# Linear attention stack: a block's projections issued beside another block's attention

## The chip, the cores and the metric

One NeuronCore of a Trainium2 chip runs the whole kernel. The metric is the device time of one execution in microseconds (us), as the median of several runs; the profile comes from one further execution. TensorE is PE in the profile (PEld is its weight load), VectorE is DVE, ScalarE is ACT, GpSimd is POOL, and SyncE (SP) issues most transfers.

## The reference, cut to what matters

A batch of 2 sequences of 2048 positions with 256 features goes through a stack of three layers with causal linear attention (16 heads of 16), and then through two layers with windowed softmax attention. All is float32. The change touches the first stack alone:

```python
for l in range(L):                       # L = 3
    q = (out @ Wq[l] + bq[l]).reshape(B, S, N_HEAD, dh)
    k = (out @ Wk[l] + bk[l]).reshape(B, S, N_HEAD, dh)
    v = (out @ Wv[l] + bv[l]).reshape(B, S, N_HEAD, dh)
    Qf = favor(q, omega[l])              # exp(+-u - |x|^2/2), u = x @ omega
    Kf = favor(k, omega[l])
    a = causal_linear_attention(Qf, Kf, v).reshape(B, S, D)
    a = a @ Wo[l] + bo[l]
    h = layer_norm(out + a, ln1_g[l], ln1_b[l])
    y = jax.nn.relu(h @ W1[l] + bf1[l]) @ W2[l] + bf2[l]
    out = layer_norm(h + y, ln2_g[l], ln2_b[l])
...
# causal_linear_attention, per head and position:
#   S += k v^T ; z += k ; out = (q S) / (q z + eps)
```

## The kernel before, in words

The stack cuts each sequence into 8 blocks of 256 positions: 16 blocks, each with 3 layers, so 48 layer steps. `favor_block` (L732) is one block's whole way and `favor_layer` (L462) one layer of it. Both are Python generators: the code up to the next `yield` issues a piece of work, and the `yield` says how much TensorE time the piece is counted for, how long the block has then to wait for other engines, which key it needs for its next piece, and which other layer step must be done before. `planned` (L91) holds four blocks at a time (`at_once`) and lets the one go on that is due first and whose key is free. A key is held by one block at a time. The order that comes out is the order of TensorE's instructions; those of the other engines are put in order by the framework, from the same program. Every engine then works through its own list.

The pieces of a layer, with the names of their tiles, as the profile shows them:

- projections: `pq` (L475) for q and k, `pv` (L491) for v, then `xs` on DVE (L486) with its squares on ACT (L487), and `vp` on DVE (L502)
- features: `pu` (L516), a product that uses the array in two column halves (128*64 in the profile), `ft` = exp on ACT (L526), `qe` on DVE (L532)
- scores: the running sum `z` (DVE L538, POOL L548), the transposes `tk` (L552) and their copy `ktm` (ACT L554), the first half of the scores `sc` (L563, rows in quarters, 32*128), masked to `att` by DVE (L569), the state update `su` (L583), masked to `sum` (DVE L591)
- second half of the scores, `den` (L611) and its reciprocal `rb` on ACT (L613, L614)
- values: `nd` from the states (L622) and from the weighted values (L635, the array in four column strips, 128*32), then `aT` on DVE (L658)
- output product `po` (L665), then the sum `s` (DVE L673) and a norm: statistics (L414, L415) on DVE, `rs` on ACT (L417, L418), `dn` on DVE (L421)
- `ntp` (L431) turns `dn`, ACT scales it (L435), POOL makes the residual `res` (L444, L445)
- the MLP in 8 pieces under the key `mlp`: `pf` (L687), relu to `fr` on ACT (L695), `acc` (L698), and behind the last one `s` (DVE L710) with a norm and `ntp`

Before the change, a block took the key `attention` ahead of its projections and gave it up behind `nd`; the projections also waited for the same layer of the sequence's previous block, whose state they do not use but the scores and values do.

PSUM is given out by tags, in turn within a tag. `mm` has three banks for pq, pv, pu, tk, su, den, nd, po and ntp. `sc` has four: a half of the scores takes all four, one for each quarter i, and each `pf` takes the next one:

```python
scs = [psum.tile([P, KT, 2, P], F32, tag="sc", name="sc", bufs=4) for _ in range(4)]
...
pf = psum.tile([P, TA], F32, tag="sc", name="pf", bufs=4)
```

`acc` has one bank, `xs` two buffers (for q and for k), and `vp` is one of two tiles that layer steps use in turn.

Behind the stack follows the softmax part, whose order is written out in a table of times (`WHEN`); the change does not touch it. The tables for it are loaded and scaled (`next_weights`, L721, `scale_tables`, L170) while the last blocks of the stack run.

Of the kernel before, what the change touches and what calls it, by code (L numbers as in the profile page):

```python
# [39 lines left out]
def block_kernel(ctx: ExitStack, tc: tile.TileContext, t: dict, out: bass.AP):  # L40
# [47 lines left out]

    done = set()

    def planned(jobs, at_once):  # L91

        jobs, live, held, now, count = iter(jobs), [], {}, 0.0, 0
        while True:
            while len(live) < at_once:
                g = next(jobs, None)
                if g is None:  # L100
                    break
                live.append([now, count, g, None, None])
                count += 1
            if not live:
                return
            e = min(
                e[:2] + [e] for e in live
                if held.get(e[3], e) is e and (e[4] is None or e[4] in done)
            )[2]
            if e[3]:  # L110
                held[e[3]] = e
            step = next(e[2], None)
            keep = step[2] if step and len(step) > 2 else None
            for k in [k for k, o in held.items() if o is e and k != keep]:
                del held[k]
            if step is None:
                live.remove(e)
                continue
            now = max(now, e[0]) + step[0]
            e[0] = now + step[1]  # L120
            e[3:] = list(step[2:]) + [None] * (4 - len(step))


    WHEN = {
# [88 lines left out]
    with ExitStack() as c1:  # L213
# [9 lines left out]
        def load_x(b, n):  # L223
            xin = work.tile([P, NCA, D], F32, tag="xin", name="xin", bufs=3)
            nc.sync.dma_start(
                xin, x_in[b, n * TA : (n + 1) * TA, :].rearrange("(c p) d -> p c d", p=P)
            )
            return xin
# [180 lines left out]
        def normed(src):  # L409

            mv = sp.tile([P, NCA, 2], F32, tag="mv", name="mv")
            for c in range(NCA):
                bs = sp.tile([P, 6], F32, tag="bs", name="bs")
                nc.vector.bn_stats(bs, src[:, c, :])  # L414
                nc.vector.bn_aggr(mv[:, c, :], bs)  # L415
            rs = sp.tile([P, NCA], F32, tag="rs", name="rs")
            nc.scalar.activation(rs, mv[:, :, 1], AF.Ln, bias=eps_t)  # L417
            nc.scalar.activation(rs, rs, AF.Exp, scale=-0.5)  # L418
            dn = work.tile([P, NCA, D], F32, tag="dn", name="dn", bufs=3)
            for c in range(NCA):  # L420
                nc.vector.tensor_scalar(  # L421
                    dn[:, c, :], src[:, c, :], mv[:, c, 0:1], rs[:, c : c + 1], ALU.subtract, ALU.mult
                )
            return dn

        def turned(dn, dst, gain, bias):

            tp = mm_tile("ntp").rearrange("p (k c) -> p k c", k=KT)
            for kt in range(KT):
                for c in range(NCA):  # L430
                    nc.tensor.transpose(  # L431
                        tp[:, kt, c * P : (c + 1) * P], dn[:, c, kt * P : (kt + 1) * P], ident
                    )
            for kt in range(KT):
                nc.scalar.activation(dst[:, kt, :], tp[:, kt, :], AF.Identity, bias=bias(kt), scale=gain(kt))  # L435

        def scaled(dn, gi, bi, plus=None):

            r = work.tile([P, NCA, D], F32, tag="res", name="res", bufs=6)
            add = brow[:, bi, :].unsqueeze(1).to_broadcast([P, NCA, D])  # L440
            if plus is not None:
                nc.gpsimd.tensor_tensor(plus, plus, add, ALU.add)
                add = plus
            nc.gpsimd.tensor_tensor(r, dn, brow[:, gi, :].unsqueeze(1).to_broadcast([P, NCA, D]), ALU.mult)  # L444
            nc.gpsimd.tensor_tensor(r, r, add, ALU.add)  # L445
            return r
# [15 lines left out]
        def favor_layer(b, n, l, h, hres):  # L462
# [38 lines left out]
            for c in range(NCA):  # L501
# [3 lines left out]
                    bvb[:, l, :].rearrange("p (i q d) -> p i q d", q=2, d=16),  # L505
                    ALU.add,
                )
            yield 5.2, 0.6, "attention"
            if callable(hres):
                hres = hres()  # L510
            feat = []
# [203 lines left out]
            h2 = hp.tile([P, KT, TA], F32, tag="h", name="h2")  # L715
            turned(dn, h2, lambda k: v("g2", k), lambda k: v("b2", k))
            hres = scaled(dn, R_G2 + l, R_B2 + l)
            yield 0.5, 0.9, "attention", (b, n - 1, l + 1) if n else None
            return h2, hres

        def next_weights():  # L721

            late.append(0)
            if len(late) == B:
                attn_w[0] = load_attn(0)
                mlp_w[0] = load_mlp(0)
            elif len(late) == 2 * B:
                scale_tables(*attn_w[0][1:4])
# [3 lines left out]
        def favor_block(b, n):  # L732
            if (b, n) == (0, 0):
                dn, h = h_first
            else:
                dn = normed(early.pop((b, n)) if (b, n) in early else load_x(b, n))
                yield 0.0, 4.0
                h = hp.tile([P, KT, TA], F32, tag="h", name="h0")
                turned(dn, h, lambda k: mod[:, 1, k, b : b + 1], lambda k: mod[:, 0, k, b : b + 1])
            hres = partial(scaled, dn, R_G0 + b, R_B0 + b)  # L740
            if n > 0:
                hres = hres()
            yield 0.5, 0.9, "attention", (b, n - 1, 0) if n else None
            for l in range(LA):
                if l == 2 and n == S // TA - 1:
                    next_weights()
                h, hres = yield from favor_layer(b, n, l, h, hres)
            if n == S // TA - 1:
                next_weights()
            x1 = scaled(h, R_GE + b, R_BE + b, load_x(b, n))  # L750
            at = n * NCA % NCH
            blk = b, n * TA // TB
            nc.sync.dma_start(xmid[blk][:, at : at + NCA, :], x1)
            dn = normed(x1)
            yield 0.0, 7.0
            hm = hp.tile([P, KT, TA], F32, tag="hm", name="hm", bufs=1)
            turned(dn, hm, lambda k: mod[:, 4, k, b : b + 1], lambda k: mod[:, 3, k, b : b + 1])
            nc.sync.dma_start(hmid[blk][:, :, at * P : at * P + TA], hm)
            yield 0.5, 0.0

        with tc.manual_schedule(engines={mybir.EngineType.PE}):
            blocks = [favor_block(b, n) for n in range(S // TA) for b in range(B)]
            with tc.issue_after(last_first):
                planned(blocks[:1] + [rest_of_setup()] + blocks[1:], 4)
# [632 lines left out]
```

## Time and profile before

| | us |
|---|---|
| median of 3 runs | 2979.69 (2979.21 to 2981.54) |
| the profiled execution | 2982.33 |
| its span on the core | 2980.5 |
| start of the last `acc` of the linear stack | 1563.2 |
| one layer step of the steady run, po to po | 31.4 |
| matmul group of four, start to next start | 0.86 |

The profile gives busy time per engine, the instructions in order of time, and for each idle stretch of an engine what ended it. A line such as `pf L687 <- DVE att L569` says that the matmul of L687 could not start until DVE had finished its instruction of L569. Ends of matmuls are modelled, and matmuls overlap, so the pace is read from start to start.

### The profile page before, as it was taken

The page shows a single profiled execution, that of the slowest core. Times are in us where ns is not written, and L with a number is a line of the kernel's source. Part 1 is how long each engine was busy: PE and PEld are TensorE (multiplying, and loading weights), DVE is VectorE, ACT ScalarE, POOL GpSimd, SP SyncE. Part 2 cuts the span into 40 slices and gives each one's busy share as a digit, 9 for nine tenths or more (in the row PEclk, how much of TensorE's full clock was granted, in tenths as well). Part 3 has the DMA queues.
Part 4 walks back from the last instruction along what each step waited for, and adds up shares of the span by engine and source line. Part 5 has one row for each costly group of instructions (what it writes and reads, how often), then busy time and mean ns, then how long its engine had stood idle before and what let it go on. Part 6 is the DMA issues. An engine that isn't in the chain of part 4 may idle for free.

```text
span 2980.5 us, 49140 instructions
## 1 busy us (share of the span) xinstructions
PE 2909.9 (98%) x19323; PEld 2128.4 (71%) x19323; DVE 1681.2 (56%) x4186; ACT 1339.6 (45%) x3263; POOL 1067.1 (36%) x942
## 2 busy tenths in 40 slices
PE   8999999999999999999996999999999999999999
PEld 6888887888888888888784777775444777776444
DVE  5555556555665556655534777774224777775222
ACT  3343344343443334343334667665114666766211
POOL 4222233222422223322324666663002666663000
PEclk9999999999999999999998999999999999999999
DMA  6000010000100001001012000001000000000011
GB/s 217 1 1 1 8 36 15 1 1 1 43 16 1 1 1 36 22 1 43 23 34 77 1 1 1 1 1 58 0 0 10 20 1 1 2 1 8 28 43 36
DMA packets 38327, 59.48 MB, mean 20 GB/s; under 512 B 3854, under 2 KB 29008, under 8 KB 37456
## 3 DMA queue, kind: packets, MB, share of 16 engines
q1 hardware_dynamic: 36288, 52.37, 5.3%
q8 instruction: 153, 2.51, 0.3%
q0 software_dynamic: 992, 2.92, 0.3%
q10 hardware_dynamic: 816, 1.05, 0.1%
q14 instruction: 78, 0.64, 0.1%
HBM read 43.72 MB, written 12.60 MB: 19 GB/s over the span
## 4 chain that ended last, share of the span: by engine, by line
PE 89%; DVE 4%; ACT 3%; POOL 2%; issue 1%; DMA 1%; ACTq 0%; POOLq 0%; DVEq 0%; SPq 0%
PE acc L698 11%; PE pf L687 10%; PE pqkv L860 10%; PE pg L1205 5%; PE pq L475 5%; PE acc L1243 5%; PE pa L1205 4%; PE av L1049 4%; PE sim L956 3%; PE ptp L1023 3%; PE po L1068 3%; PE nd L635 3%; PE sc L563 3%; PE pu L516 3%; PE po L665 3%; PE pv L491 3%
## 5 line engine op out<-in xcount | busy, mean ns | idle before, releaser
L698 PE MATMUL acc<-wb,fr 128*128 128x256 f32 x1536 | 398.5, 382 | 7.0 <-ACT fr L695 5.1
L687 PE MATMUL pf<-h,wa 128*128 128x256 f32 x1536 | 402.4, 385 | 0.6 <-DVE att L569 0.3
L695 ACT ACTIVATE fr<-pf,vec 128x256 f32<-128x256 f32 x384 | 180.6, 471 | 427.1 <-PE pf L687 426.3
L860 PE MATMUL pqkv<-wqkv,s 128*128 128x512 f32 x768 | 357.3, 601 | 6.5 <-DMA s<-h 6.5
L569 DVE TENSOR_TENSOR att<-sc,cst 128x512 f32<-128x512 f32 x384 | 238.3, 683 | 158.0 <-PE sc L563 158.0
L698 PEld LDWEIGHTS acc<-wb,fr 128*128 128x128 f32 x1536 | 288.8, 190 | 54.0 <-ACT fr L695 8.6
L444 POOL TENSOR_TENSOR res<-dn,brow 128x512 f32<-128x512 f32 x112 | 145.1, 1295 | 486.0 <-DVE dn L421 479.4
L687 PEld LDWEIGHTS pf<-h,wa 128*128 128x128 f32 x1536 | 277.3, 191 | 55.5 <-issue 19.8
L1011 POOL TENSOR_TENSOR pm<-pm,sum 128x1024 f32<-128x1024 f32 (+1 forms) x128 | 235.5, 1840 | 179.6 <-DVE sum L1006 179.6
L996 ACT ACTIVATE pm<-pm,mx 128x256 f32<-128x256 f32 (+1 forms) x512 | 249.4, 488 | 59.2 <-DVE mx L988 59.0
L860 PEld LDWEIGHTS pqkv<-wqkv,s 128*128 128x128 f32 x768 | 138.0, 193 | 133.9 <-issue 132.0
L902 POOL TENSOR_TENSOR rot<-raw,rsn_wo 128x512 f32<-128x512 f32 x128 | 160.3, 1273 | 180.8 <-ACT raw L883 180.5
L1214 DVE SCALAR_TENSOR_TENSOR ge<-pa,vec,ge 128x512 f32<-128x512 f32 x80 | 60.1, 751 | 282.9 <-PE pa L1205 231.6
L1213 ACT ACTIVATE ge<-pg,vec 128x512 f32<-128x512 f32 x96 | 65.8, 685 | 316.5 <-PE pg L1205 316.5
L487 ACT ACTIVATE xs<-xs 64x512 f32<-64x512 f32 x192 | 120.6, 628 | 152.3 <-DVE xs L486 143.0
L1205 PE MATMUL pg<-s,w 128*128 128x512 f32 (+1 forms) x384 | 182.2, 597 | 0.0
L475 PE MATMUL pq<-h,wa 128*128 128x256 f32 x768 | 176.2, 383 | 0.7 <-ACT h L435 0.7
L486 DVE TENSOR_TENSOR xs<-pq,vec 64x512 f32<-64x512 f32 x192 | 132.1, 688 | 75.3 <-PE pq L475 71.5
L1243 PE MATMUL acc<-ge,w 128*128 128x512 f32 (+1 forms) x384 | 168.8, 600 | 0.0
L475 PEld LDWEIGHTS pq<-h,wa 128*128 128x128 f32 x768 | 146.7, 192 | 22.6 <-issue 1.4
L924 POOL TENSOR_TENSOR qk<-qk,rot 128x1024 f32<-128x1024 f32 x64 | 151.3, 2363 | 0.5
L1205 PE MATMUL pa<-s,w 128*128 128x512 f32 x320 | 150.4, 592 | 0.0
(163 smaller groups left out, 5339.7 us busy)
## 6 DMA issues: line engine op xcount, KB each, us to landing
xin<-in_x_dram SPq DMA_DIRECT2D x32, 256.0 KB, 2.8
x<-res SPq DMA_DIRECT2D x16, 256.0 KB, 2.1
h<-hm SPq DMA_DIRECT2D x16, 256.0 KB, 2.4
s<-h SPq DMA_DIRECT2D x16, 256.0 KB, 4.8
xl<-x SPq DMA_DIRECT2D x8, 512.0 KB, 4.3
out_dram<-res SPq DMA_DIRECT2D x8, 512.0 KB, 3.2
w<-in_w_dram SPq DMA_DIRECT2D x6, 640.0 KB, 3.9
wa<-in_W_dram SPq DMA_DIRECT2D x3, 1024.0 KB, 8.3
```

The costliest lines, as they stand in the source:

```text
L475: nc.tensor.matmul(pq[:, g, :], W[wn, l][:, kt, g * P : (g + 1) * P], h[:, kt, :], start=(kt == 0), stop=(kt == KT - 1),)
L569: nc.vector.tensor_tensor(am, scs[i].rearrange("p g q c -> p (g q) c"), caus.unsqueeze(1).to_broadcast([P, 2 * KT, P]), ALU.mult,)
L687: nc.tensor.matmul(pf, W["W1", l][:, kt, f * P : (f + 1) * P], h1[:, kt, :], start=(kt == 0), stop=(kt == KT - 1),)
L695: nc.scalar.activation(fr[f], pf, AF.Relu, bias=v("bf1", f))
L698: nc.tensor.matmul(acc[:, c, :], fr[f - 1][:, c * P : (c + 1) * P], W["W2", l][:, f - 1, :], start=(f == 1 and c == 0), stop=(f == NF), sk ...
L860: nc.tensor.matmul(pq, s[:, kt * TB + c * P : kt * TB + (c + 1) * P], wqkv[:, kt, i * INNER : (i + 1) * INNER], start=(kt == 0), stop=(kt ...
L902: nc.gpsimd.tensor_tensor(rot[:, :, :, lo : lo + 32], got["raw"][:, :, :, hi : hi + 32], rsn[:, ti, :, lo : lo + 32].unsqueeze(2).to_broad ...
L924: nc.gpsimd.tensor_tensor(got["qk"], got["qk"], got["rot"], ALU.add)
L996: nc.scalar.activation(pm[:, hd, :], pm[:, hd, :], AF.Exp, bias=of("mx", hg)[:, hd : hd + 1], accum_out=of("sum", hg)[:, hd : hd + 1],)
L1011: nc.gpsimd.tensor_tensor(pm, pm, of("sum", hg).unsqueeze(2).to_broadcast([P, 4, kw]), ALU.mult)
L1205: nc.tensor.matmul(pt[:m, :], w1[:, kt, off : off + m], hb[:, kt * TB : (kt + 1) * TB], start=(kt == 0), stop=(kt == KT - 1),)
L1243: nc.tensor.matmul(acc[m], w2[rs_, f, m * P : (m + 1) * P], g[rs_, :], start=(f == 0), stop=(f == NFH - 1),)
```

## The change

Keys become sets. A block takes `projections` for its projections, and the wait for the previous block's layer step moves behind them: to the piece that makes the features, for which the block needs `projections` and `attention` together. After the features it gives `projections` up, so that another block may project while this one attends. A block that is due for `mlp` while another holds it brings the holder forward by `LEAD` (8 us of the planner's time). The last three places of the diff are, in order: behind the projections in `favor_layer`, at its end, and in `favor_block` ahead of the first layer.

```diff
+    LEAD = 8.0
+
     def planned(jobs, at_once):
...
-                live.append([now, count, g, None, None])
+                live.append([now, count, g, (), None])
                 count += 1
             if not live:
                 return
+
+            ahead = {
+                k for e in live for k in e[3]
+                if e[0] <= now and held.get(k, e) is not e and k == "mlp"
+            }
             e = min(
-                e[:2] + [e] for e in live
-                if held.get(e[3], e) is e and (e[4] is None or e[4] in done)
+                [e[0] - (LEAD if ahead & set(e[3]) else 0.0), e[1], e] for e in live
+                if all(held.get(k, e) is e for k in e[3]) and (e[4] is None or e[4] in done)
             )[2]
-            if e[3]:
-                held[e[3]] = e
+            held.update((k, e) for k in e[3])
             step = next(e[2], None)
-            keep = step[2] if step and len(step) > 2 else None
-            for k in [k for k, o in held.items() if o is e and k != keep]:
+            keep = step[2].split() if step and len(step) > 2 else ()
+            for k in [k for k, o in held.items() if o is e and k not in keep]:
                 del held[k]
...
-            e[3:] = list(step[2:]) + [None] * (4 - len(step))
+            e[3:] = keep, step[3] if len(step) > 3 else None
...
-            yield 5.2, 0.6, "attention"
+            yield 5.2, 0.6, "projections attention", (b, n - 1, l) if n else None
...
-            yield 0.5, 0.9, "attention", (b, n - 1, l + 1) if n else None
+            yield 0.5, 0.9, "projections"
...
-            yield 0.5, 0.9, "attention", (b, n - 1, 0) if n else None
+            yield 0.5, 0.9, "projections"
```

## The prediction

> **What bounds the kernel now.** I read the page first, then the busy time by stretches, then TensorE's waits, then the instructions of the linear stack in order of time.
>
> The page:
>
> ```profile
> span 2980.5 us, 49140 instructions
> PE   2909.9 (98%) x19323; PEld 2128.4 (71%) x19323; DVE 1681.2 (56%) x4186; ACT 1339.6 (45%) x3263; POOL 1067.1 (36%) x942
> ```
>
> TensorE is the bound. The change touches the linear stack alone, which ends at about 1565 us, and there TensorE is busy for 1537.5 of 1565 us; from 200 to 1400 us for 1192.5 of 1200, at a granted clock of 1.00. So this stage can gain only what TensorE loses between its matmuls, and it loses as soon as TensorE is made to wait. The view of its waits (columns: total us, times, longest) has little in that stack:
>
> ```profile
> PE ntp L431 <- DVE dn L421: 13.3, 4, 7.8
> PE acc L698 <- ACT fr L695: 5.1, 5, 1.2
> PE den L611 <- POOL z L548: 4.1, 1, 4.1
> PE tk L552 <- ACT ft L526: 3.1, 4, 0.9
> PE acc L698 <- DVE s L710: 1.8, 1, 1.8
> PE pf L687 <- DVE att L569: 0.3, 1, 0.3
> ```
>
> Now one layer step of the steady run, in order of time (start, us, engine, line). First TensorE, then VectorE (DVE):
>
> ```profile
> 599.90 1.03 PE L698 MATMUL acc<-wb,fr 128*128 128x256 f32 x4
> 600.86 1.95 PE L516 MATMUL pu<-xs,omt 128*64 128x256 f32 x16
> 602.73 1.13 PE L687 MATMUL pf<-h,wa 128*128 128x256 f32 x4
> 603.70 1.03 PE L698 MATMUL acc<-wb,fr 128*128 128x256 f32 x4
> 604.56 0.60 PE L552 MATMUL tk<-cst,ft 128*128 128x128 f32 x4
> 605.09 1.15 PE L563 MATMUL sc<-qe,ft 32*128 32x256 f32 x16
> 606.17 1.16 PE L583 MATMUL su<-vp,ktm 128*128 128x128 f32 x8
> 607.16 1.03 PE L687 MATMUL pf<-h,wa 128*128 128x256 f32 x4
> ```
>
> ```profile
> 606.26 2.48 DVE L569 TENSOR_TENSOR att<-sc,cst 128x512 f32<-128x512 f32 x4 [1.31 <-PE sc L563]
> 618.52 0.76 DVE L710 TENSOR_TENSOR s<-acc,res 128x256 f32<-128x256 f32 x2 [0.27 <-PE acc L698]
> 620.76 0.74 DVE L421 TENSOR_SCALAR dn<-s,mv,rs 128x256 f32<-128x256 f32 x2 [0.60 <-ACT rs L418]
> 621.41 0.75 DVE L673 TENSOR_TENSOR s<-po,res 128x256 f32<-128x256 f32 x2
> ```
>
> Start to start gives the pace: a group of four plain matmuls (acc at 603.70 to tk at 604.56) takes 0.86, but acc before pu takes 0.96, and pf after pu 0.97. Going into and out of a group that uses part of the array (128*64 or 32*128) costs about 0.1 us each time. Second reading: after the scores (sc) VectorE starts the mask products (att) 0.09 after su has begun, so the first is done (606.26 + 0.68, the page's mean of L569) before pf wants its PSUM bank at 607.16. scores and pf share four banks (tag "sc"); pf after su gets the bank of the first score, so it cannot start until the first att is done. Here that hides with 0.2 us to spare.
>
> **The change, part by part.** In the instruction order of the two built programs, 35 of 48 layer steps now have pu right behind nd of the other block (before: none). A steady step of before is pu, pf acc, tk, sc, su, pf acc, pf acc, sc, den, pf acc, nd, acc pf, po, pf acc, ntp, pf acc, pq pv, ntp, pf acc. After it is pu, pf acc, ntp, **po, tk, sc, su, pf** acc, pq pv, ntp, pf acc, pf acc, sc, den, pf acc, pf acc, pf acc acc, pf, nd, then the next pu. The counts of instructions are equal on TensorE. What matters is VectorE's queue: before it runs qe, z, att x4, sum, att x4, aT, then the two norms (each s, statistics, dn), xs, vp. After it runs qe, z, **s of po with its whole norm (L673, L414, L415, L421), then att x4**, sum, xs, vp, att x4, s of acc with its norm, aT. The output product po has moved to just before tk, and its norm stands ahead of the masks in an engine that takes them in this order.
>
> *Cost 1, the first mask is late.* Call P the end of po, when tk starts. TensorE goes on: tk 0.53 (604.56 to 605.09), sc 1.08, su 0.99, so pf wants to run at P + 2.60. VectorE: with the engine idle, s of po starts 0.20 after the next group on TensorE (442.43 and 442.63 in this trace: the pair below). The norm takes from 618.52 to 621.41, 2.89, of which 0.60 waits for ScalarE's rs; ScalarE has only ktm (0.59) in front of it. The first att then takes 0.68: done at P + 3.77. How pf comes back from such a wait is shown once, where VectorE was late with att for another reason:
>
> ```profile
> 442.43 1.03 PE L698 MATMUL acc<-wb,fr 128*128 128x256 f32 x4
> 442.63 0.76 DVE L673 TENSOR_TENSOR s<-po,res 128x256 f32<-128x256 f32 x2 [3.30 <-PE po L665]
> ```
>
> ```profile
> 1223.80 1.88 DVE L569 TENSOR_TENSOR att<-sc,cst 128x512 f32<-128x512 f32 x3
> 1224.53 1.13 PE L687 MATMUL pf<-h,wa 128*128 128x256 f32 x4 [0.30 <-DVE att L569]
> 1225.50 1.03 PE L698 MATMUL acc<-wb,fr 128*128 128x256 f32 x4
> ```
>
> pf starts 0.05 after the first att (1223.80 + 0.68), and its group then takes 0.97 instead of 0.86, so 0.10 more. Hence pf starts at P + 3.82 instead of P + 2.60: 1.22 + 0.10 = 1.32 us for each such step. Queued behind pf are acc, pq and pv, the whole TensorE stream: nothing hides it. Po directly before tk, sc, su, pf occurs in 34 steps, 31 of them as above: 31 x 1.32 = 40.9. Three (one in each later round over the blocks) have one more pair of statistics in front (0.74 and 0.30 of L414 and L415, about 0.9 net): 3 x 2.2 = 6.6. Three more steps have another norm between z and att, with no po: VectorE needs, from the start of pu, 1.8 to the first ft, qe 0.88, dn twice 0.65, z 1.3, statistics 0.9, the gap 0.60, dn 0.65, att 0.68 = 8.1, where pf wants to run at 6.3: 3 x 1.9 = 5.7. In three steps pq stands behind su instead, and pv waits about 0.2 for sum: 0.6. Together 53.8. Bounds: without the slower restart 1.2 a step; with POOL working beside dn a dn pair took 1.03 instead of 0.74 (at 623.64), so 1.6. POOL's order has nothing there in the steady steps, so I take 1.32.
>
> *Gain 1, nd to pu.* No row shows this pair. A group such as pu costs, over plain matmuls at 0.108 each: 0.10 on the way in, 1.88 - 1.73 = 0.15 in it, 0.10 in the next group, 0.35 in all. Joined, two such islands become one. If going from 128*32 to 128*64 cost nothing 0.35 would go; if each still pays all, 0. I take half, 0.17, since one way in and one way out are gone and one change of shape stays: 35 x 0.17 = 6.0, between 0 and 12.3.
>
> [...]
>
> *Gain 2, waits that go.* tk now stands behind pu, pf, acc, ntp and po (about 3.9 after pu) instead of 1.83, so its wait for ft goes: 3.1. At the start the next block's pq and pv (5.2) stand between pu and den, and cover den's wait for POOL, whose queue there hangs on a transfer that lands whenever it does (its first sums wait for brow): 4.1. Around 1480 to 1488 TensorE waited 1.8 for s and 2.9 for dn, and came back at half pace (clock 0.56 between 1485 and 1490), while the tables for the next stage were scaled; that scaling is still in the last steps, so I take 3 of a possible 7. Together 10, between 0 and 15. The chain that ends the stack (7.8 for dn) is unaltered.
>
> *Small.* acc twice behind one pf occurs in most steps: its fr is ready 0.73 after pf (ScalarE 0.47 plus hand-overs) against 0.86; three such places of before lost 0.03 each: 35 x 0.03 = 1.
>
> xs, vp, qe, z and ft have their readers done before they are written again in the new order, and SP's queue carries the same loads at nearly the same places: nothing for these; if xs were late, pu would wait, but pq stands some 20 us ahead of it.
>
> Sum: 53.8 - 6.0 - 10 + 1 = +38.8, span 2980.5 to about 3019. The profiled execution took 2982.3 and the runs' median is 2979.7, 0.8 under the span, so the time is 2979.7 + 38.8 = 3018.5.
>
> **Rivals.**
> *A, the wait is not there* (faster): pf gets another bank, or VectorE is done in time. For it: everywhere else the new order leaves more time (att of the second scores has 8 us before nd instead of 4). Against: pf at 607.16 has 0.2 us of slack, and the norm in front takes 2.89. The point from which it decides: the norm must take under 1.6. Then -6.0 - 10 + 1 = -15: 2965.
> *B, half of it*: the norm of po overlaps so far (statistics of the first half starting before po ends) that 0.45 a step stays: 34 x 0.45 = 15, which the gains cancel: 2980. Against: s waits for the whole po in the row above.
> *C, the waits cool the array*: 1.3 us of idle every 32 us drop the clock, as at 1485. A four-matmul group at half pace loses 0.86, four of them 3.4: 31 x 3.4 = 105 on top: 3124. Against: a wait of 1.23 (for fr, at 373.73) left the next group at 0.97 and the clock at 1.00.
> *D, longer norms*: dn beside POOL, 1.6 a step, and no gain 2: 31 x 0.29 + 10 = 19 more: 3037.
>
> **How the numbers follow.** Forecast 0.78, A 0.06, B 0.04, C 0.02, D 0.10. The predicted time is the forecast's, 3018. Its own range is 3005 to 3030 (gain 1 from 0 to 12, gain 2 from 0 to 15). To leave no more than 2 in 10 out the range goes to D and half way to B: 3000 to 3037. A change under 0.2% (6 us) can't be told from none; faster 0.06, same 0.04, slower 0.90.
>
> **What would show it.** Right: TensorE's waits list pf (L693 in the new numbering) for DVE att some 37 times, about 40 us in all with the weight load's share; in the timeline each steady step shows a gap before pf behind su, and VectorE goes from dn of po to att without idling; the step grows from 31.4 to about 32.5 us; pu comes 1.9 after nd begins, with no plain group between. Wrong: no idle before that pf, or pf waiting for something else (ScalarE's fr, xs), or a clock under 1.0 in the steady run. The largest single risk is the 1.32, which multiplies by 31.

## The result, and the profile after

The changed kernel takes 3054.76 us (median of 6 runs, 3051.24 to 3059.04), the kernel before 2979.61 in the same session: a ratio of 1.0252, 95% interval [1.0239, 1.0266]. The forecast was 3018 us, with a range of 3000 to 3037. Its sign was right and its size about half: +38.8 us foretold, +71.7 found between the two profiled spans. Lines of code from 100 on have moved down by 6.

The page after, with the costliest group of TensorE (its columns: busy us and mean ns, then the idle time just before, with what ended it):

```profile
span 3052.2 us, 49026 instructions
PE 2921.5 (96%) x19323; PEld 2137.3 (70%) x19323; DVE 1690.2 (55%) x4186; ACT 1347.8 (44%) x3263; POOL 1068.5 (35%) x942
...
L693 PE MATMUL pf<-h,wa 128*128 128x256 f32 x1536 | 410.6, 390 | 71.2 <-DVE att L575 70.5 <-ACT h L441 0.7
```

The engines do the same work, and TensorE, which bounds the kernel, stands idle for 130.7 us of the span instead of 70.6. Its waits after the change, longest sums first (total us, times, longest):

```profile
PE pf L693 <- DVE att L575: 70.5, 41, 6.4
...
PE ntp L437 <- DVE dn L427: 8.3, 2, 7.8
...
PE po L671 <- DVE aT L664: 5.8, 4, 1.7
```

The waits that the change was to remove are gone (`tk` for `ft`, `den` for POOL). The new first line was 0.3 us before and holds 70.5 now. One steady step after, in order of time (start, us, engine, line), TensorE and then VectorE:

```profile
595.65 1.95 PE L641 MATMUL nd<-att,vp 128*32 128x128 f32 x64
597.53 1.95 PE L522 MATMUL pu<-xs,omt 128*64 128x256 f32 x16
...
601.68 1.89 PE L671 MATMUL po<-wb,aT 128*128 128x256 f32 x8
603.41 0.60 PE L558 MATMUL tk<-cst,ft 128*128 128x128 f32 x4
...
605.01 1.16 PE L589 MATMUL su<-vp,ktm 128*128 128x128 f32 x8
607.23 1.13 PE L693 MATMUL pf<-h,wa 128*128 128x256 f32 x4 [1.05 <-DVE att L575]
```

```profile
600.28 1.38 DVE L544 TENSOR_TENSOR_SCAN z<-ft,zl,zero 128x256 f32<-128x256 f32 x2
603.61 0.76 DVE L679 TENSOR_TENSOR s<-po,res 128x256 f32<-128x256 f32 x2 [1.95 <-PE po L671]
...
605.84 0.73 DVE L427 TENSOR_SCALAR dn<-s,mv,rs 128x256 f32<-128x256 f32 x2 [0.60 <-ACT rs L424]
606.49 2.48 DVE L575 TENSOR_TENSOR att<-sc,cst 128x512 f32<-128x512 f32 x4
```

This is the forecast's picture to the hundredth of a microsecond: `pu` follows `nd`, po ends at P = 603.41, VectorE puts s and the norm ahead of the mask, and `pf` starts at P + 3.82.

The total, split by the starts of `pu` (step k runs from the k-th `pu` to the next), shows where the forecast went wrong; a steady step in the tables below is the median of the 23:

| part | before | after | difference |
|---|---|---|---|
| start to first pu, steps 1 to 5 | 156.1 | 161.8 | +5.7 |
| 23 steady steps (6-11, 18-23, 30-35, 42-46) | 721.5 | 747.4 | +25.9 (1.12 a step) |
| steps 12-17, 24-29, 36-41 (blocks change) | 583.0 | 628.4 | +45.4 (14.5, 16.7, 14.2) |
| step 47 and all that follows | 1519.8 | 1514.6 | -5.2 |

The steady steps lose what was foretold. The eighteen steps in which one pair of blocks gives way to the next (three rounds of six) lose 2.5 us each, more than twice as much. In each round TensorE waits for 12.5 us in all, in six places, where it waited for 2.1 to 2.8 before. Here is the longest of these waits, on TensorE, and VectorE's and GpSimd's work up to its end:

```profile
819.26 1.16 PE L589 MATMUL su<-vp,ktm 128*128 128x128 f32 x8
826.77 2.08 PE L693 MATMUL pf<-h,wa 128*128 128x256 f32 x4 [6.36 <-DVE att L575]
828.64 1.91 PE L704 MATMUL acc<-wb,fr 128*128 128x256 f32 x4
830.35 1.06 PE L437 MATMUL ntp<-cst,dn 128*128 128x128 f32 x4
```

```profile
817.21 2.70 DVE L427 TENSOR_SCALAR dn<-xin,mv,rs 128x256 f32<-128x256 f32 x2
819.84 2.34 DVE L544 TENSOR_TENSOR_SCAN z<-ft,zl,zero 128x256 f32<-128x256 f32 x2
822.10 0.72 DVE L420 BATCH_NORM_STATS2 bs<-res 128x6 f32<-128x256 f32 x2
...
823.64 2.48 DVE L427 TENSOR_SCALAR dn<-res,mv,rs 128x256 f32<-128x256 f32 x2 [0.60 <-ACT rs L424]
826.04 2.47 DVE L575 TENSOR_TENSOR att<-sc,cst 128x512 f32<-128x512 f32 x4
```

```profile
816.98 1.45 POOL L450 TENSOR_TENSOR res<-dn,brow 128x512 f32<-128x512 f32 x1 [15.49 <-DVE dn L427]
818.50 1.26 POOL L451 TENSOR_TENSOR res<-res,xin 128x512 f32<-128x512 f32 x1
819.99 1.64 POOL L450 TENSOR_TENSOR res<-dn,brow 128x512 f32<-128x512 f32 x1 [0.23 <-DVE dn L427]
821.71 1.52 POOL L451 TENSOR_TENSOR res<-res,brow 128x512 f32<-128x512 f32 x1
...
823.44 1.26 POOL L554 TENSOR_TENSOR z<-ft,z 128x512 f32<-128x512 f32 x1
824.66 1.31 POOL L448 TENSOR_TENSOR xin<-xin,brow 128x512 f32<-128x512 f32 x1
```

Two things are to be seen. A pair of `dn` takes 2.70 and 2.48 us where the steady step has 0.73, and `z` 2.34 instead of 1.38, while GpSimd makes residuals (L448 to L451) and its product for `z` (L554). And after the wait the `pf` group takes 1.87 from start to start instead of 0.97, `acc` 1.71 instead of 0.86: TensorE has come back at half pace. The clock that was granted to it (PEclk) was 0.50 between 825.5 and 829.0 us.

### The profile page after: what moved, and what is told of

The parts are those of the page before. It is cut to its first block, busy times and chain, and to the rows that moved or that the text cites. A ratio compares the mean times of both kernels' runs of the same rounds, so it can differ in the third digit from the quotient of the medians.

```text
span 3052.2 us, 49026 instructions
## 1 busy us (share of the span) xinstructions
PE 2921.5 (96%) x19323; PEld 2137.3 (70%) x19323; DVE 1690.2 (55%) x4186; ACT 1347.8 (44%) x3263; POOL 1068.5 (35%) x942
## 3 DMA queue, kind: packets, MB, share of 16 engines
q10 hardware_dynamic: 816, 1.05, 0.1%
## 4 chain that ended last, share of the span: by engine, by line
PE 83%; DVE 9%; ACT 3%; POOL 2%; issue 1%; DMA 1%; SPq 0%; DVEq 0%; ACTq 0%; POOLq 0%
PE pf L693 11%; PE acc L704 10%; PE pqkv L866 10%; PE pg L1211 5%; PE pq L481 5%; PE acc L1249 5%; PE pa L1211 4%; PE av L1055 4%; PE sim L962 3%; PE ptp L1029 3%; PE po L1074 3%; PE pv L497 3%; PE po L671 2%; PE nd L641 2%; PE pu L522 2%; PE sc L569 2%
## 5 line engine op out<-in xcount | busy, mean ns | idle before, releaser
L693 PE MATMUL pf<-h,wa 128*128 128x256 f32 x1536 | 410.6, 390 | 71.2 <-DVE att L575 70.5
L450 POOL TENSOR_TENSOR res<-dn,brow 128x512 f32<-128x512 f32 x112 | 144.7, 1292 | 444.7 <-DVE dn L427 437.6
L662 POOL TENSOR_TENSOR st<-sth,sum 128x256 f32<-128x256 f32 x42 | 30.8, 734 | 512.4 <-PE nd L628 512.2
L716 DVE TENSOR_TENSOR s<-acc,res 128x256 f32<-128x256 f32 x96 | 36.2, 418 | 217.0 <-PE acc L704 217.0
```

What stands on the lines that cost most here:

```text
L693: nc.tensor.matmul(pf, W["W1", l][:, kt, f * P : (f + 1) * P], h1[:, kt, :], start=(kt == 0), stop=(kt == KT - 1),)
```

## The experiments

Fifteen kernels ran, each beside the kernel before on the same chip. This table has their profiles by the parts used above (steps 1 to 5 from the first `pu`; us), and each one's ratio to before with its interval. Two values stand where steady steps fall into two groups:

| kernel | steps 1-5 | a steady step | 12-17 | 24-29 | 36-41 | ratio |
|---|---|---|---|---|---|---|
| before | 136.8 | 31.39 | 194.0 | 194.0 | 195.0 | 1 |
| after | 141.4 | 32.51 | 208.6 | 210.7 | 209.2 | 1.0252 [1.0239, 1.0266] |
| masks_first | 144.7 | 31.20 | 213.8 | 212.2 | 212.2 | 1.0192 [1.0176, 1.0207] |
| five_banks | 135.2 | 31.53 | 209.5 | 209.8 | 207.5 | 1.0151 [1.0135, 1.0167] |
| no_pool_sums | 138.4 | 32.51 | 203.1 | 202.0 | 200.8 | 1.0135 [1.0120, 1.0150] |
| lead_zero | 129.8 | 31.39 | 194.3 | 194.3 | 195.2 | 0.9983 [0.9973, 0.9992] |
| all_norms | 146.1 | 31.21 | 213.6 | 214.2 | 214.4 | 1.0235 [1.0218, 1.0252] |
| lead_alone | 149.7 | 33.21 | 203.1 | 198.8 | 202.1 | 1.0217 [1.0197, 1.0237] |
| before_plus6 | 162.7 | 33.28, 34.97 | 223.9 | 223.6 | 225.9 | 1.0581 [1.0560, 1.0602] |
| before_plus9 | 166.4 | 34.21, 35.89 | 233.5 | 233.4 | 236.8 | 1.0814 [1.0792, 1.0835] |
| no_stats_before | 134.8 | 31.39 | 193.7 | 193.7 | 194.5 | 0.9967 [0.9955, 0.9979] |
| no_stats_after | 130.8 | 31.19 | 199.8 | 199.8 | 198.2 | 0.9981 [0.9972, 0.9991] |
| after_scalar_dn | 136.6 | 31.19 | 197.2 | 197.2 | 197.2 | 1.0021 [1.0011, 1.0030] |
| scalar_po | 133.8 | 31.19 | 207.6 | 208.2 | 208.9 | 1.0106 [1.0090, 1.0123] |
| scalar_x | 141.3 | 32.51 | 203.1 | 203.3 | 203.1 | 1.0208 [1.0194, 1.0223] |
| scalar_po_x | 136.4 | 31.19 | 199.7 | 199.7 | 199.7 | 1.0044 [1.0030, 1.0058] |
| lead_zero_scalar_dn | 131.2 | 32.11 | 194.8 | 194.8 | 194.7 | 1.0056 [1.0042, 1.0070] |

**masks_first**: the sum and norm of po are issued behind the first four masks.

```diff
...
-            for c in range(NCA):
-                nc.vector.tensor_tensor(s[:, c, :], po[:, c, :], hres[:, c, :], ALU.add)
-            dn = normed(s)
+            later.append((s, po, hres, got := []))
             yield 1.7, 3.8
+            if not got: flush()
+            dn = got[0]
...
             att = [scores(0)]
+            with tc.issue_after(last_mask[0]): flush()
```

> The changed kernel with the same order on TensorE; on VectorE alone, the sum and the norm behind po are traced behind the next first masks and issued behind the last of them (34 steps). Theory (VectorE takes its list in order, and pf waits for the bank of the first mask): the 1.06 us wait of pf and its slow restart go, a steady step falls from 32.51 to about 31.2 us, and the 2.0 us waits of three later steps go with the clock they cost; the three waits of 6.4 us stay. Total about 3003 us (2995 to 3012). Rival (the wait only moves: the norm is now about 3 us later, and ntp behind pv or po waits for it instead): step 32 to 32.5, total 3040 to 3055.

Measured: 3036.93 us. The steady step went to 31.20, which is 0.19 under the kernel before: the wait is gone and what is left is the gain of `pu` behind `nd`. The 23 steady steps bear the theory out; the total does not, since the steps around a change of blocks got worse (213.8, 212.2, 212.2 against 208.6, 210.7, 209.2). The waits moved there:

```profile
PE ntp L436 <- DVE dn L427: 35.6, 11, 7.8
PE pf L701 <- DVE att L583: 28.0, 8, 6.4
```

`ntp`, the transpose of a norm put back too far, now waits (2.8 us twice a round), and a 6.4 us wait for the masks stays, behind norms that this kernel did not move.

**five_banks**: five PSUM banks for the scores and `pf`, two for the rest (three before).

```diff
...
-                scs = [psum.tile([P, KT, 2, P], F32, tag="sc", name="sc", bufs=4) for _ in range(4)]
+                scs = [psum.tile([P, KT, 2, P], F32, tag="sc", name="sc", bufs=5) for _ in range(4)]
...
```

> The changed kernel with five PSUM banks for scores and pf and two for the rest, instead of four and three; TensorE's order the same, and VectorE's in the steady steps. Theory (pf waits for the one bank that the first mask still reads): pf behind su takes the fifth bank and does not wait; steady step 31.2 to 31.6, as two banks may make su or pv wait a few tenths; total 3000 to 3020 us. Rival (pf waits for VectorE for another reason than its bank): step 32.5, total 3050 or more.

Measured: 3024.92 us, 5 over the theory's range. A steady step is 31.53: `pf` finds a bank and does not wait, so the reused bank is how VectorE's lateness reaches TensorE. With two banks in the other tag, `pu`, `pv`, `pq` and `su` wait instead (10.0, 6.5, 5.2 and 3.9 us in all), and in the steps around a change of blocks nothing is won.

**no_pool_sums**: the residual's gain and bias on GpSimd are left out; ScalarE copies dn instead, so later values differ.

```diff
-            nc.gpsimd.tensor_tensor(r, dn, brow[:, gi, :].unsqueeze(1).to_broadcast([P, NCA, D]), ALU.mult)
-            nc.gpsimd.tensor_tensor(r, r, add, ALU.add)
+            nc.scalar.copy(r, dn)
```

> The changed kernel with the residual's gain and bias left out: in place of GpSimd's product and sum a copy on ScalarE (112 times), so the residual path has other values. The order on TensorE is the same. Theory (GpSimd's two passes slow VectorE's dn and z that run beside them, 4.7 of the 6.4 us of the long wait): in the three long steps dn falls from 2.5 us a pair to 0.74, z from 2.3 to 1.4, the wait of pf from 6.4 to about 1.7 us, and TensorE's clock stays at 1.00 in these steps; the steady wait of 1.06 stays. Total 3025 to 3038 us. Rival (the order alone makes the long wait): it stays above 5 us, total 3048 to 3058.

Measured: 3019.3 us, 6 better than the theory allowed. The steady steps are as in the changed kernel (32.51); the eighteen others lose 5.5, 8.7 and 8.4 us less. So half of the 45.4 us that were lost in these steps comes from GpSimd's work on the residuals beside VectorE. At the place shown above `dn<-xin` takes 0.73 and z 1.38 us here, and `pf` waits 2.6 us instead of 6.4:

```profile
803.97 0.73 DVE L427 TENSOR_SCALAR dn<-xin,mv,rs 128x256 f32<-128x256 f32 x2
804.61 1.38 DVE L543 TENSOR_TENSOR_SCAN z<-ft,zl,zero 128x256 f32<-128x256 f32 x2
...
807.46 1.68 DVE L427 TENSOR_SCALAR dn<-res,mv,rs 128x256 f32<-128x256 f32 x2 [0.60 <-ACT rs L424]
```

```profile
809.79 1.73 PE L692 MATMUL pf<-h,wa 128*128 128x256 f32 x4 [2.62 <-DVE att L574]
```

The theory had `pf` wait 1.7 us there; `dn<-res` still takes 1.68 us, beside GpSimd's product for z, which was left in.

**lead_zero**: the lead set to nothing, the rest of the change as it is.

```diff
-    LEAD = 8.0
+    LEAD = 0.0
```

> The changed kernel with LEAD = 0: the keys are still sets, but a waiting block no longer brings the MLP forward. nd is then followed by pu in 6 steps instead of 35, and po stands before tk in 6 instead of 38. Theory (the loss comes from po standing right before tk, and that from LEAD): a steady step is as before the change, 31.4 us; total 2975 to 2990 us. Rival (the split of the keys costs by itself): over 3010 us.

Measured: 2973.19 us, 0.9983 [0.9973, 0.9992]: slightly faster than before. The split of the keys costs nothing. Without the lead, po goes back to its old place behind `nd`, the steady step is that of before, `pu` follows `nd` in 6 steps instead of 35, and steps 1 to 5 are 7.0 us shorter than before: the gain that the forecast looked for at the start lies in the keys.

**lead_alone**: the lead of 8 with the one key of before.

```diff
-            yield 5.2, 0.6, "projections attention", (b, n - 1, l) if n else None
+            yield 5.2, 0.6, "attention"
...
```

> The lead of 8 kept, but with the one key of before (attention) in place of the two, so that a block's projections don't run beside the other's attention and pu doesn't follow nd. In the order po then stands right before pu, not before tk: VectorE has pu's 1.9 us and a pf and acc more for the sum and norm of po before the masks are due. Theory (the lead costs only because it puts po right ahead of tk): no wait for masks in the steady steps, span 2975 to 2995. Rival (any order with po led forward makes VectorE late): pf waits for att again in most steps, span above 3015.

Measured: 3043.64 us; the theory fell and its rival held. The steady step is 33.21. It is not po that stands badly here but the sum of `acc`, which the lead brings to just before the second masks:

```profile
654.68 0.76 DVE L716 TENSOR_TENSOR s<-acc,res 128x256 f32<-128x256 f32 x2 [7.99 <-PE acc L704]
...
657.56 2.48 DVE L575 TENSOR_TENSOR att<-sc,cst 128x512 f32<-128x512 f32 x4
```

```profile
654.57 1.15 PE L569 MATMUL sc<-qe,ft 32*128 32x256 f32 x16
655.65 1.13 PE L617 MATMUL den<-z,cst 128*128 128x256 f32 x4
658.30 1.13 PE L693 MATMUL pf<-h,wa 128*128 128x256 f32 x4 [1.52 <-DVE att L575]
```

The pattern is the same: a norm (2.9 us) that VectorE starts when the scores are about to land delays the mask by more than what TensorE has to put between, here `den` alone. One row of the wait list (`pf` for `att`) has two different culprits in two kernels.

**before_plus6 and before_plus9**: the kernel before, with six and with nine VectorE operations put ahead of the masks.

```diff
+            for _ in range(6):
+                du = sp.tile([P, KT, TA], F32, tag="du", name="du", bufs=1)
+                nc.vector.tensor_scalar(du, qf, 1.0, None, ALU.mult)
             zsum[b, l] = sp.tile([P, KT], F32, tag=f"z{b}{l}", name="zl")
```

> The kernel before, with six VectorE operations of 128x512 (some 0.44 us each, 2.64 us in all, written to a tile nobody reads) put ahead of the first masks of every step; TensorE's order is that of before. There the first mask starts 1.31 us after VectorE is free, so pf should begin to wait by 2.64 - 1.31 = 1.33 us less some 0.2. Theory (late masks alone explain the change's steady steps): pf waits 1.0 to 1.4 us in nearly all of 48 steps, a steady step takes 32.4 to 32.8 instead of 31.39, the span is 3025 to 3045. Rival (the steady loss came from TensorE's new order): the step stays within 0.3 of 31.39 and the span below 2995.

> The same with nine such operations, eight of which stand ahead of the first mask: 3.5 us, so the wait should be 2.0 to 2.4 us a step. Theory of a plain wait: a steady step takes 31.39 plus the wait, 33.4 to 33.8, and every group of matmuls after it keeps its pace (pf 0.86, acc 0.86); span 3070 to 3095. Rival (a wait of some 2 us slows TensorE's clock after it, as in steps 24 and 25 of after): the step takes 1 to 3 us more than before's plus its wait, groups after the wait show 1.1 to 1.9, the granted clock falls below 0.97, and the span passes 3110.

Measured: 3151.99 and 3221.42 us. Late masks alone, with TensorE's old order, make `pf` wait 46 and 47 times, as the theory has it; but the sizes were far too small (3025 to 3045 and 3070 to 3095 us were expected). Five of the operations, beside GpSimd's product for z, took 3.2 us, so that the wait was 1.63 us in a steady step of the first kernel and 2.56 in most of the second's, instead of 1.0 to 1.4 and 2.0 to 2.4. In four of the six steps around a change of blocks it was 3.5 to 5.9 and 4.4 to 7.3 us, for which the theory had no term. And some steps took 1.69 us more than others with the very same wait. Two such steps of before_plus6 (TensorE in order of time):

```profile
681.71 1.13 PE L690 MATMUL pf<-h,wa 128*128 128x256 f32 x4 [1.63 <-DVE att L572]
682.67 1.03 PE L701 MATMUL acc<-wb,fr 128*128 128x256 f32 x4
683.54 1.03 PE L690 MATMUL pf<-h,wa 128*128 128x256 f32 x4
...
714.99 1.67 PE L690 MATMUL pf<-h,wa 128*128 128x256 f32 x4 [1.64 <-DVE att L572]
716.46 1.91 PE L701 MATMUL acc<-wb,fr 128*128 128x256 f32 x4
718.16 1.38 PE L690 MATMUL pf<-h,wa 128*128 128x256 f32 x4
```

and the granted clock (PEclk, third from the right) in windows around both:

```profile
682.00:685.50 3.50, 3.50 (x20) 2.81 (x23) 2.04 (x4) 0.95 (x2) 0.72 (x1) 1.00 0.00 0
712.60:715.40 2.80, 1.16 (x9) 0.95 (x9) 2.73 (x5) 0.00 (x0) 0.54 (x1) 1.00 0.00 0
715.40:718.80 3.40, 3.40 (x10) 2.69 (x9) 1.93 (x4) 0.47 (x1) 0.72 (x1) 0.51 0.02 7
```

After the second wait TensorE runs at half its clock for 3.4 us, which costs half of that, 1.7 us; after the first it does not. The rival for the clock, which the forecast had as its case C, is true of some waits and not of others (see the last section). So is the rival that stood against a plain wait in before_plus9: 14 of its 23 steady steps take 34.2 us, the other nine 35.6 to 37.5.

**all_norms**: as masks_first, and the norm of a new block's input stands behind the first masks too, the norm of a block's last features behind the second; po ahead of a block's last features keeps its norm in front.

```diff
...
             att = [scores(0)]
+            with tc.issue_after(last_mask[0]): flush(False)
...
             att.append(scores(1))
+            with tc.issue_after(last_mask[0]): flush()
...
+            if l == 2 and b == 0: flush(False)
             yield 1.7, 3.8
+            if not got: flush()
+            dn = got[0]
...
-            dn = normed(x1)
+            later.append((x1, None, None, got := [], False))
...
```

> Sums and norms behind the masks, all of them: as in masks_first, the residual sum of po and its norm follow the first four masks in VectorE's order; now the norm of a new block's input does too, the norm of a block's last features follows the second four masks, and only the po before a block's last features keeps its norm ahead of the masks. masks_first took the wait out of the steady steps (31.20 us there, 0.19 less than before) but left 213 us in the six steps around each change of blocks, where before takes 194. Theory (what is lost there is the lateness of the masks behind the other norms, 6.4 us once a round with the slow clock after it, and 2.8 us twice where a transpose waited for a norm put back too far): the six steps fall to 196 to 203, the span to 2985 to 3005. Rival (TensorE's new order itself is bad in these steps, or GpSimd holds VectorE up whatever its order): the six steps stay above 207 and the span above 3018.

Measured: 3048.39 us. The theory, that a better order on VectorE would win the eighteen steps back, fell, and its rival's numbers came: they take 213.6, 214.2 and 214.4. The waits of `pf` shrink once more, and the transposes take them over:

```profile
PE ntp L436 <- DVE dn L427: 45.7, 17, 7.9
PE pf L703 <- DVE att L584: 20.3, 16, 2.7
```

In these steps TensorE's new order asks for the masks and for the norms within the same few microseconds, and whichever VectorE does last is waited for. That left two readings: VectorE has too much to do there, or TensorE's order is bad in itself.

**no_stats_after and no_stats_before** tell them apart. The statistics of the stack's norms are left out of both kernels (dn becomes the sum less 0.125, times 0.5, so later values differ); the order of TensorE is unaltered in each.

```diff
-                nc.vector.bn_stats(bs, src[:, c, :])
-                nc.vector.bn_aggr(mv[:, c, :], bs)
...
-                    dn[:, c, :], src[:, c, :], mv[:, c, 0:1], rs[:, c : c + 1], ALU.subtract, ALU.mult
+                    dn[:, c, :], src[:, c, :], 0.125, 0.5, ALU.subtract, ALU.mult
```

> The changed kernel with the statistics of the LayerNorms in the linear stack left out (no mean, no variance, no root: dn is the sum less 0.125, times 0.5, so all later values differ). It takes 0.74 + 0.30 us of VectorE, some 0.6 us of ScalarE and the wait between the two off each norm; TensorE's instructions and their order are those of the change. all_norms showed that moving a norm only moves the wait in the six steps around a change of blocks; this takes the time away. Theory (the change's loss is VectorE's late answers: it must give a norm and four masks within a stretch of TensorE's new order that is shorter than both): pf no longer waits in the steady steps, which take 31.2 us (31.39 before, less 0.19 for pu behind nd); the six steps take 194 to 200; the span is 2970 to 2992, and stands within -8 to +18 us of no_stats_before. Rival (the order itself costs TensorE time, by changes of tile shape or by transposes that come too early): it stays more than 35 us above no_stats_before.

> The control: the kernel before with the same statistics left out. VectorE was in nobody's way there but for a few waits at the start and the end of the stack, so both theories expect little: a steady step of 31.39 within 0.05, a span of 2965 to 2980.

Measured: 2974.02 and 2969.17 us. With VectorE relieved (of the statistics and of the wait for ScalarE's `rs`), the distance between the two orders falls from 75 us to 5. Some 70 us of the loss are therefore VectorE's late answers. In the steady steps the new order gains 0.20 us (31.19 against 31.39). In the eighteen steps it still loses 6.1, 6.1 and 3.7 us, but each round still has 5.8 us of waits for VectorE (`pf` for masks 4.2, `po` for `aT` 1.6): a cost of TensorE's order by itself is not seen.

**after_scalar_dn** gives the same relief with nothing left out: the last step of each norm goes to ScalarE.

```diff
+            nb = sp.tile([P, NCA], F32, tag="nb", name="nb")
+            nc.scalar.activation(nb, mv[:, :, 0], AF.Identity, scale=-1.0)
             for c in range(NCA):
-                nc.vector.tensor_scalar(
-                    dn[:, c, :], src[:, c, :], mv[:, c, 0:1], rs[:, c : c + 1], ALU.subtract, ALU.mult
+                nc.scalar.activation(
+                    nb[:, c : c + 1], nb[:, c : c + 1], AF.Identity, scale=rs[:, c : c + 1]
+                )
+                nc.scalar.activation(
+                    dn[:, c, :], src[:, c, :], AF.Identity, bias=nb[:, c : c + 1], scale=rs[:, c : c + 1]
                 )
```

> The changed kernel with the last step of each norm, dn, on ScalarE instead of VectorE (an Identity with a scale and a bias, for which three tiny operations work out minus the mean times rs). Nothing is left out. It takes 0.73 us and the 0.60 us wait for rs off VectorE per norm and puts some 1.6 us on ScalarE. Theory (VectorE's answer is what is late): 1.79 us of norm instead of 3.1 now stand ahead of the masks, so that pf waits 0.2 to 0.4 us instead of 1.06 in a steady step, which takes 31.4 to 31.7; the six steps around a change of blocks take 199 to 206; span 2985 to 3012. Rival (ScalarE's added time makes acc wait for its features, or the transposes for dn): steady step above 32.3 or the six steps above 210, span above 3035.

Measured: 2985.25 us, 69.5 less than the changed kernel, and 1.0021 of before; a steady step (31.19) and the six steps (197.2) came out a little below what the theory allowed. In its waits the 70.5 us have become 8.7:

```profile
PE pf L698 <- DVE att L580: 8.7, 11, 4.2
...
PE su L594 <- ACT ktm L565: 5.1, 13, 1.1
```

**scalar_po, scalar_x and scalar_po_x** split that: dn on ScalarE for po's norm alone (the first line below), for the norms of a new block's input and of a block's last features alone (the second, and its like), and for all three.

```diff
-            dn = normed(s)
+            dn = normed(s, True)
             yield 1.7, 3.8
...
-            dn = normed(x1)
+            dn = normed(x1, True)
```

> As after_scalar_dn, but only the norm of po's sum has its dn on ScalarE; the norms of acc's sum, of a new block's input and of a block's last features keep it on VectorE. In after_scalar_dn a steady step took 31.19 us and the six steps around a change of blocks 197.2 (32.51 and 208.6 to 210.7 in the changed kernel). Theory (in the six steps it is the norms of the new block's input and of the old block's features that make the masks late, which the prediction priced at 1.9 us each): steady steps at 31.2, the six steps still above 205, span 3003 to 3020. Rival (po's norm alone decides there too): the six steps below 201, span below 2995.

> The complement: only the norms of a new block's input and of a block's last features have dn on ScalarE. Theory: steady steps stay at 32.5, the six steps fall to 198 to 204, span 3018 to 3034. Rival: the six steps stay above 206, span above 3040.

> Both: all norms but that of acc's sum. ScalarE has less to do than in after_scalar_dn. Theory: steady steps at 31.2, the six steps at 195 to 200, and the waits for ScalarE at the start of the stack (2.0 and 2.3 us in after_scalar_dn) partly gone: span 2972 to 2988. Rival (the norm of acc's sum, still on VectorE, now holds the second masks up): the six steps above 203, span above 2995.

Measured: 3011.37, 3039.81 and 2992.07 us. po's norm is all of the steady loss (31.19 against 32.51) and little of the eighteen steps' (0.9, 2.5 and 0.3 us won). The two others are nothing in the steady steps and win 5.5, 7.4 and 6.1 us in the eighteen; all three together win 8.9, 11.0 and 9.5, and acc's norm, which after_scalar_dn adds, another 2.5 each. scalar_x came out 6 us over the theory's range, since `acc` then waits for ScalarE (7.3 us in all), scalar_po_x 4 over.

**lead_zero_scalar_dn**: the same edit on the fastest version.

> lead_zero, the fastest version so far (2973 us, 0.9983 of before), with dn on ScalarE as in after_scalar_dn. In its order VectorE has little that is late: leaving the statistics out of the kernel before gave 0.9967, so at most about 11 us are there to be had. Theory: a steady step stays at 31.39 and a part of the waits at the start and the end goes; span 2960 to 2973. Rival (ScalarE's features come late behind dn, acc waits): span above 2978.

Measured: 2994.89 us, 21.7 slower than lead_zero; the rival held, by another wait than it named:

```profile
PE pq L486 <- ACT h L446: 12.5, 25, 2.2
```

There po's norm follows acc's closely and `pq` stands soon behind the transposes; ScalarE has a second dn to make (1.09 us, at 627.42) before it scales `h` (1.00, at 628.42). The edit that gives one order 69.5 us takes 21.7 from the other. Of the versions that compute everything lead_zero stays the fastest, 0.17% under the kernel before.

## Why the prediction had the sign and half of the size

*Cost 1, the 31 steps*: right for 29 of them, which wait 1.05 or 1.06 us; the other two stand at the end of the stack (see Gain 2). It priced 1.32 us a step less 0.17 for `pu` behind `nd`, so 1.15; the steady steps lost 1.12, by the route described: a bank that waits for its mask (five_banks), a mask that waits for po's norm (masks_first, scalar_po).

*"Three more steps have another norm between z and att, with no po ... 3 x 1.9"*: this step failed. They waited 6.36 us each. The term added up dn at 0.65 twice, z at 1.3 and the rest, durations of a VectorE that is alone, and took "POOL's order has nothing there in the steady steps" over to steps that are not steady. There GpSimd makes the residuals of two blocks and its product for z: by their rows, from start to start, dn took 2.63 and 2.40 and z 2.26, which is 1.98 + 1.75 + 0.96 = 4.7 us more; 1.9 + 4.7 = 6.6, against 6.36 found. no_pool_sums shows GpSimd's part (2.6 us of the wait are left at this place), scalar_x the norms' (1.5 to 1.6 left). The forecast had seen the slowed dn once (1.03 against 0.74), and used it only for the steady steps, as a bound and in rival D.

*"Three steps have one more pair of statistics in front ... 2.2"*: the wait was 1.99, 2.00 and 2.00 in the three rounds, but in the second and third the clock fell after it (PEclk 0.52 between 771.0 and 774.4 us in the second) and the step took 1.70 us more than in the first (53.86 against 52.16). What stood in front was not a pair of statistics but a dn of the old block, between the two halves of z (765.39 us in the second round, 0.71 us), so that s began later.

*What had no term*: `pf` waiting 1.5 for the second masks behind acc's norm (458.80 in the first round), `po` waiting 1.4 for aT, and the clock after long waits. The changed kernel has eleven windows of 3.4 us at half clock between its third and last `pu`, the kernel before two: 9 x 1.7 = at most 15 us, since TensorE idled in part of them. By its own prices the forecast had 3 x (2.2 + 1.9 + 1.3 + 0.2 - 0.5) = 15 us for the eighteen steps; they cost 45.4. That is 30 of the 33 us by which the forecast fell short.

*Gain 1*, 0.17 us for each `pu` behind `nd`: 0.19 (masks_first) and 0.20 (no_stats_after) a step. The half that was taken between nothing and 0.35 is about right. It fits one way in and one way out that are gone (0.10 us each in the forecast's rows); what the change of shape that is left costs was not measured by itself.

*Gain 2*, 10 us: the waits named did go, and lead_zero has 7.0 us of them at the start; in the changed kernel steps 3 to 5 gave them back (+15.8 against -10.1 up to step 2), and the end of the stack, where 5.2 were won, has new waits of 5.7 and 3.0 us for masks while the tables are scaled.

*Rivals.* A (the wait is not there) is what the steady steps of no_stats_after show once VectorE is quick enough; its 2965 is not shown by that kernel's 2974, since the kernel before without statistics takes 2969. C was given 2 in 100: the clock does fall, but behind waits of 1.6 us and more, and there not always; never behind the 1.06 us ones for which it was priced. D named the right mechanism, dn beside POOL, in the wrong steps.

## What to carry to other kernels

When an order of the bound engine is changed, the question for each moved product is which answer of another engine it triggers, and what that engine must answer next: a product whose follow-up takes 2.9 us must not stand 2.6 us ahead of one whose answer is needed at once. Price the irregular steps (first, last, changes of blocks) from their own rows, with what the neighbouring engines do there; a steady step's durations do not hold in them (here 0.73 us for a pair of `dn` in the one, 2.70 in the other). And where moving an operation only moves the wait (in all_norms `pf` waits 20.3 us instead of 70.5, `ntp` 45.7 instead of 8.3), the engine has too much to do in that stretch: take work off it, and try the same edit anew in each order.

## What was not expected of the hardware

*VectorE beside GpSimd's products.* In the linear stack of the changed kernel a VectorE operation that lies beside GpSimd tensor_tensors for at least nine tenths of its time takes, by the median, 1.29 instead of 0.41 us (`dn`, 6 instances against 207 with no GpSimd product beside them), 1.68 instead of 0.73 (`z`, 6 against 84) and 1.19 instead of 0.48 (`qe`, 8 against 53). The masks (0.68, 108 instances), the statistics (0.41, 34), `s` (0.42, 8) and `xs` (0.69, 8) are not slowed. dn's 0.41 becomes about the 1.27 us of one GpSimd product (the median of `res`). So `dn`, `z` and `qe` were the rows of the forecast that were in danger; why these are slowed and the others are not, no run shows.

*The clock falls after about half a window of idling.* The granted clock changes at edges that are multiples of 3.41 us apart (in the changed kernel it fell at 771.14 and rose at 774.55 us). Over the seventeen profiles, between the third and the last `pu`, a full-clock window of this length in which TensorE idled for less than a share of 0.45 was never followed by one at half clock; from 0.60 up it always was (77 of 77); in between 23 of 79 were. The least idle share that was followed is 0.479, the largest that was not 0.581. In the changed kernel alone six such windows, of shares from 0.56 to 1.00, were followed by half clock, and none up to 0.50 was. So a wait of 1.06 us (a share of 0.31) never cost here, and one of 1.63 cost 1.69 more in some steps and nothing in others, by where it fell against the edges. By the same count a wait of over 4.1 us should always cost: this is an estimate, from one window getting at least 0.6 of idling (half of 4.1 us, of 3.41) however the wait lies.
